# A three-layer graph network on one core: how far back a gather's hold reaches, ten or twelve gathered pairs

## The chip, the cores and the metric

The kernel runs on one core of one Trainium2 chip. The metric is the device time of one execution in microseconds, from launch to the last output written. The core's engines are TensorE (PE in the profile, PEld for its weight loads), VectorE (DVE), ScalarE (ACT), GpSimd (POOL) and SyncE (SP). Each has a queue of its own that it works through in order; they meet through semaphores. Transfers between the chip's memory (HBM) and the core's on-chip memory (SBUF) go through 16 DMA engines that all queues share. POOL issues the indirect transfers (an index for each row), SP and ACT the plain ones.

## The reference

N = 6250 nodes with D = 256 features, E = 100000 edges with 32 attributes and one of three types. The edges come sorted by their destination. Three layers follow each other, then a layernorm:

```python
ew = edge_attr @ edge_w + edge_b
rel_masks = [(edge_type == i).astype(x.dtype) for i in range(3)]
inv_cnt = [1.0 / jnp.maximum(segment_sum(m, dst), 1.0) for m in rel_masks]
for l in range(3):
    residual = x
    msg = relu(x[src] * ew)
    out = zeros((n, D))
    for i in range(3):
        h = segment_sum(msg * rel_masks[i][:, None], dst) * inv_cnt[i][:, None]
        out = out + h @ weights[l, i]
    out = out + x @ roots[l] + biases[l]
    x = residual + relu(out)
# result: layernorm(x_in + x)
```

`x[src]` is one row of 1 KB for each edge, in each of the three layers: this is what the gathers fetch.

## The kernel before

**Pairs and quads.** 128 edges are a tile, two tiles a pair (256 edges), two pairs a quad. There are 391 pairs. A pair is the unit of a step, a quad that of most DVE and ACT instructions. Pairs are numbered by u; a quad's number is q = u // 2, and i (0 or 1) is the tile within a pair.

**Layers and their order.** `layer()` writes out the program of one layer, once for each of the three. `order_of` lists the pairs in the order in which their sums are made. In layer 0 all 391 pairs are gathered. There, 26 quads (the destinations with the most edges, spread among the others) also write their edge weights into a table in HBM, `zone_table`, sorted anew. Layers 1 and 2 read these edges back sorted by source as 75 "lots" with plain loads, and gather only the other 339 pairs; they have 414 steps. `fetched` is the list of the gathered pairs in this order, and `nth[u]` is a pair's place in it.

**A step.** The loop over `it` (L1086) writes the instructions of all engines, and the engines keep this order. At step `it`, `pair(k)` is the pair k places ahead in the order. The parts that matter here, in the order in which they are written:

- `reduce(pair(0))`, L897 to L925: PE sums the pair's weighted rows into their nodes by a one-hot matrix. The last matmul of each tile is remembered as `summed[u, i]`.
- `gather(pair(AHEAD))`, AHEAD = 10: POOL gathers the rows of the pair ten steps ahead, with two indirect DMAs of 128 rows (L1458), one for each tile. The target is a "room" of SBUF for a quad; eight rooms (ROWS = 8, sixteen pairs) are used in turn. In layer 0 each gather is followed by a scatter of 128 rows into `zone_table` (L757), where one is waiting; there are 104, four for each of the 26 quads.
- `weigh` of the quad whose first pair is WEIGH = 2 steps ahead: DVE multiplies the gathered rows by the edge weights (L873), ACT applies the relu (L874). The last quad is done pair by pair and tile by tile (L873, L879).
- In layer 0, `keep_ew` one step before the weighing: ACT copies the quad's edge weights from PSUM into a buffer of the pool `keep` (three buffers, KEEP = 3), from L800 or L806. From there they go to HBM, by a plain store of SP or, for the 26 quads, by four scatters of POOL. A copy must wait until the buffer's last reader, a store or four scatters, is done with it.
- `seed_ew` (L821, L824) prepares the PSUM of a quad to come, in layers 1 and 2 from `ew_s`, which SP loads from HBM (L786, 128 rows of 4 KB). `take` (L930) copies a finished group of sums from PSUM, on ACT.

**What a gather waits for.** A gather raises one of POOL's eight semaphores, and so waits until the one eight before it has landed. Its room must be free, which means that the quad sixteen pairs back has been summed. Beyond these, `hold` adds a wait by hand for a sum that is more recent than the room requires:

```python
def hold(got, u, i):
    g = nth[u]
    if g >= LEAD + HEAD:
        behind(got, fetched[g - (LEAD if g >= 2 * LEAD else LEAD + HEAD)], i)
```

`behind(got, u, i)` makes the gather `got` wait for `summed[u, i]`. With LEAD = 10 and HEAD = 2 the first 12 gathered pairs of a layer have no hold, the next 8 wait for the sum twelve gathered pairs back, and from the 21st on for that ten back. `hold_early` does the same for the first EARLY = 8 pairs of layers 1 and 2, whose gathers stand at the end of the layer before (16 in each of these layers, listed as `src_e`); for these `fetched[nth[u] - LEAD]` counts back from the list's end. In layer 0 six pairs (FIRST) are gathered ahead of the loop.

Of the kernel before, what the change touches and what calls it, by code (L numbers as in the profile page):

```python
# [442 lines left out]
def ordered_path(ctx, tc, x, attr_laid, A, weights, roots, biases, edge_w, edge_b, out, src, src_i, seg, place_i, consts, x_root,  # L443
# [249 lines left out]
    def layer(l, r_sb, b_sb, ats, early, ready, pools):  # L693
# [46 lines left out]
# [5 lines that stand above are left out]
        def behind(got, u, i):  # L745
            tc.add_manual_dep(got.ins, summed[u, i].ins.name, mybir.DependencyInfo(
                mybir.DependencyClass.Sync, mybir.DependencyReason.DATA))

        def hold_early(got, u, i):
            behind(got, fetched[nth[u] - LEAD], i)  # L750

# [463 lines left out]
PARTS = 3  # L1215
FIRST = 6
EARLY = 8
LEAD = 10
HEAD = 2
READY = 2  # L1220
LOAD_EW = 10
# [465 lines left out]
```

## Time and profile before

| | |
|---|---|
| time, median of 3 runs | 3497.67 us |
| lowest and highest | 3482.07 and 3502.85 us |
| the profiled execution | 3495.29 us |
| its span, as the profile shows it | 3493.3 us |
| mean granted TensorE clock | 0.876 |
| gathers of layer 0 in the loop (L1458, `src_io`) | 770 |
| gathers of layers 1 and 2 in the loop (L1458, `src_r`) | 1324 |
| scatters of layer 0 (L757) | 104 |

The span is the time from the first to the last instruction that the profile recorded; the execution's own time has 2.0 us more around it. A busy time counts what an engine executes; the rest is waiting. For a group of instructions the profile gives the engine's idle time just ahead of them, split up by what ended it: "issue" is time in which nothing that the profile shows was waited for, a line with an engine is the instruction that came last by the semaphores, and "remote" is a semaphore whose origin the profile could not find.

### The profile page before, as it was taken

The page shows a single profiled execution, that of the slowest core. Times are in us where ns is not written, and L with a number is a line of the kernel's source. Part 1 is how long each engine was busy: PE and PEld are TensorE (multiplying, and loading weights), DVE is VectorE, ACT ScalarE, POOL GpSimd, SP SyncE. Part 2 cuts the span into 40 slices and gives each one's busy share as a digit, 9 for nine tenths or more (in the row PEclk, how much of TensorE's full clock was granted, in tenths as well). Part 3 has the DMA queues.
Part 4 walks back from the last instruction along what each step waited for, and adds up shares of the span by engine and source line. Part 5 has one row for each costly group of instructions (what it writes and reads, how often), then busy time and mean ns, then how long its engine had stood idle before and what let it go on. Part 6 is the DMA issues. An engine that isn't in the chain of part 4 may idle for free. (4 is left out here: it accounts for less than half of the span.)

```text
span 3493.3 us, 45265 instructions
## 1 busy us (share of the span) xinstructions
PE 2595.5 (74%) x12880; PEld 1999.6 (57%) x12880; DVE 1897.1 (54%) x4221; ACT 1891.7 (54%) x2580; POOL 2137.0 (61%) x2254
## 2 busy tenths in 40 slices
PE   5778777777777687777777777776777877778766
PEld 2445455555555455555566667665566666667665
DVE  6656555656555464444445555543445555566655
ACT  5666655555555555555554455554555655555555
POOL 6666666666666665666655566665666655565664
PEclk9889888888889899898988898888898999898888
DMA  7888555555555566767666676665776767766764
GB/s 247 274 261 257 189 179 182 177 174 174 173 172 173 165 194 220 229 215 223 211 202 205 203 224 216 216 212 160 257 235 219 230 220 223 227 215 222 225 216 153
DMA packets 358718, 730.97 MB, mean 209 GB/s; under 512 B 59082, under 2 KB 215804, under 8 KB 358332
## 3 DMA queue, kind: packets, MB, share of 16 engines
q1 hardware_dynamic: 243840, 426.68, 36.1%
q0 software_dynamic: 107616, 294.11, 28.4%
q10 hardware_dynamic: 7004, 7.19, 0.7%
q8 instruction: 107, 1.75, 0.2%
q14 instruction: 151, 1.24, 0.1%
HBM read 570.29 MB, written 157.46 MB: 208 GB/s over the span
## 5 line engine op out<-in xcount | busy, mean ns | idle before, releaser
L1458 POOL DMA_INDIRECT xs<-x_mid,src_r x1324 | 1255.9, 949 | 819.8 <-issue 396.8
L1458 POOL DMA_INDIRECT xs<-in_x_dram,src_io x770 | 734.3, 954 | 455.5 <-issue 161.8
L874 ACT ACTIVATE xs<-xs 128x1024 f32<-128x1024 f32 x533 | 560.4, 1051 | 767.1 <-DVE xs L873 484.5
L922 PE MATMUL h_p<-oh,xs 128*128 128x120 f32 x4608 | 716.1, 306 | 227.9 <-DVE acc L962 79.8
L922 PEld LDWEIGHTS h_p<-oh,xs 128*128 128x128 f32 x4608 | 671.7, 216 | 300.8 <-issue 115.7
L873 DVE TENSOR_TENSOR xs<-ew_p,xs 128x1024 f32<-128x1024 f32 x533 | 643.6, 1211 | 109.3 <-issue 48.9
L962 DVE TENSOR_TENSOR acc<-h_p,acc 128x240 f32 (+1 forms) x761 | 339.9, 449 | 662.7 <-remote 201.5
L991 PE MATMUL o_p<-w_sb,acc 128*128 128x256 f32 (+1 forms) x1752 | 505.3, 431 | 108.9 <-DVE acc L962 35.3
L991 PEld LDWEIGHTS o_p<-w_sb,acc 128*128 128x128 f32 (+1 forms) x1752 | 360.4, 216 | 209.9 <-issue 64.6
L914 PE MATMUL h_p<-xs,oh 128*120 128x256 f32 x1176 | 324.6, 409 | 80.9 <-ACT oh L886 24.9
L1022 DVE SCALAR_TENSOR_TENSOR x_root<-o_p,inv,x_root 128x256 f32<-128x256 f32 (+1 forms) x438 | 211.1, 482 | 303.4 <-PE o_p L991 93.3
L821 ACT ACTIVATE ew_p<-ew_s 128x1024 f32<-128x1024 f32 (+1 forms) x340 | 343.7, 1011 | 5.9 <-DMA ew_s<-ew_all 5.0
L914 PEld LDWEIGHTS h_p<-xs,oh 128*120 128x120 f32 x1176 | 222.6, 198 | 135.5 <-issue 50.4
L806 ACT ACTIVATE keep<-ew_p 128x1024 f32<-128x1024 f32 x170 | 172.4, 1014 | 202.0 <-remote 80.6
L850 PE MATMUL ew_p<-x_root,at 64*128 64x512 f32 x606 | 199.6, 738 | 79.1 <-issue 39.0
L911 PE MATMUL h_p<-xs,oh 128*120 128x257 f32 x772 | 213.4, 406 | 59.9 <-issue 36.6
L874 ACT ACTIVATE zone<-zone 128x1024 f32<-128x1024 f32 (+1 forms) x78 | 78.7, 1009 | 323.5 <-issue 156.6
L914 PE MATMUL h_p<-zone,oh 128*120 128x256 f32 x576 | 178.0, 447 | 99.8 <-ACT zone L874 36.8
L1008 ACT ACTIVATE acc<-zero_o 128x768 f32<-128x768 f32 (+1 forms) x150 | 141.4, 943 | 139.3 <-PE o_p L991 48.7
L836 PE MATMUL ew_p<-x_all,hot 128*128 128x256 f32 x588 | 164.5, 428 | 66.7 <-DVE hot L829 34.3
L890 DVE TENSOR_SCALAR oh<-iota_w,seg_o 128x120 f32<-128x120 f32 x782 | 207.8, 328 | 0.0
L911 PEld LDWEIGHTS h_p<-xs,oh 128*120 128x120 f32 x772 | 138.0, 191 | 109.3 <-issue 59.8
(182 smaller groups left out, 2870.3 us busy)
## 6 DMA issues: line engine op xcount, KB each, us to landing
ew_s<-ew_all SPq DMA_DIRECT2D x338, 512.0 KB
ew_all<-keep SPq DMA_DIRECT2D x169, 512.0 KB
oh_l<-oh_all SPq DMA_DIRECT2D x338, 120.0 KB
zone<-zone_table SPq DMA_DIRECT2D x72, 516.0 KB
xs<-x_mid,src_r POOLq DMA_INDIRECT x1324
oh_all<-oh_b SPq DMA_DIRECT2D x169, 120.0 KB
zone_table<-blank SPq DMA_DIRECT2D x21, 677.2 KB
x_mid<-x_all SPq DMA_DIRECT2D x98, 128.0 KB
```

The costliest lines, as they stand in the source:

```text
L821: nc.scalar.activation(ew_ps[q][:, :n], ew_ss[q][:, :n], AF.Copy)
L850: nc.tensor.matmul(ew_ps[q][:, k].rearrange("p i d -> p (i d)"), at[half, :], ew_sb[half].rearrange("p i d -> p (i d)"), start=False, stop ...
L873: nc.vector.tensor_mul(there, ew_ps[q][:, pairs.start:pairs.stop, :n], there)
L874: nc.scalar.activation(there, there, AF.Relu)
L890: nc.vector.tensor_scalar(ohs[q][:, i, :], iota_w[:, :, :WIN], at, None, op0=ALU.is_equal)
L911: summed[u, i] = nc.tensor.matmul(h_p[:WK, :D + 1], ohs[u // 2][:, t, :], wide[u // 2][:, u % 2, i, :], start=(i == 0 and first), stop=(i ...
L914: summed[u, i] = nc.tensor.matmul(h_p[:WK, :D], ohs[u // 2][:, t, :], rows_of(u, i), start=(i == 0 and first), stop=(i == n - 1 and closes ...
L922: summed[u, i] = nc.tensor.matmul(h_p[:, d * WK:(d + 1) * WK], rows_of(u, i)[:, d * P:(d + 1) * P] if d < DC else full_ones, (ohs if d < D ...
L962: nc.vector.tensor_tensor(there, h_ps[span][:, :CH * WK].rearrange("p (c r w) -> p c r w", c=CH, r=R), there, op=ALU.add)
L991: nc.tensor.matmul(o_p[:n, j, :], acc[:, d, r, slot:slot + n], w_sb[:, r * DC + d, :], start=(d == 0), stop=(d == DC - 1))
L1022: nc.vector.scalar_tensor_tensor(root, o_p[:n, j, :], inv[:n, c, r:r + 1], root, op0=ALU.mult, op1=ALU.add)
L1458: got = nc.gpsimd.indirect_dma_start(out=xs[:, u % 2, i, :], out_offset=None, in_=x_rows[:, :], in_offset=bass.IndirectOffsetOnAxis(ap=src ...
```

## The change

One number is changed. The hold now reaches twelve gathered pairs back from the 25th gathered pair of a layer on, in place of ten from the 21st on; before that it reaches fourteen back (LEAD + HEAD) in place of twelve, and the first 14 gathered pairs in place of 12 have none. In `hold_early` the sum waited for is two gathered pairs further back too. Rooms, steps and AHEAD stay as they are.

```diff
 EARLY = 8
-LEAD = 10
+LEAD = 12
 HEAD = 2
```

No instruction is added, removed or moved on any engine. What changes is what they wait for. In the rows below a name after "waits" is a semaphore: DMASW0 to DMASW7 are the landings of POOL's transfers, DMAHW those of SP's and ACT's, and PE, DVE, Activation the progress of an engine. Which value of it is waited for is not shown, so nearly all gathers read alike before and after, and two places show something. The first is POOL at the beginning of layer 0, around the gathers of the 13th and the 14th pair:

```order
 L1458 DMA xs<-in_x_dram,src_io 128x256 [waits DMASW6_49]
 L1458 DMA xs<-in_x_dram,src_io 128x256 [waits DMASW7_49]
-L1458 DMA xs<-in_x_dram,src_io 128x256 [waits DMASW0_49,PE_49]
-L1458 DMA xs<-in_x_dram,src_io 128x256 [waits DMASW1_49,PE_49]
-L1458 DMA xs<-in_x_dram,src_io 128x256 [waits DMASW2_49,PE_49]
-L1458 DMA xs<-in_x_dram,src_io 128x256 [waits DMASW3_49,PE_49]
+L1458 DMA xs<-in_x_dram,src_io 128x256 [waits DMASW0_49]
+L1458 DMA xs<-in_x_dram,src_io 128x256 [waits DMASW1_49]
+L1458 DMA xs<-in_x_dram,src_io 128x256 [waits DMASW2_49]
+L1458 DMA xs<-in_x_dram,src_io 128x256 [waits DMASW3_49]
 L1458 DMA xs<-in_x_dram,src_io 128x256 [waits DMASW4_49,PE_49]
 L1458 DMA xs<-in_x_dram,src_io 128x256 [waits DMASW5_49,PE_49]
```

These four gathers no longer wait for a sum; they stand in the same place.

The second is ACT in layer 0, behind one of the 26 quads whose weights are scattered: the third and the fourth copy into `keep` after that quad's own (both L806 here). Before:

```order
L806 ACTIVATE keep<-ew_p 128x1024 [waits DMAHW3_49,PE_49,Activation_49]
L824 ACTIVATE ew_p<-x_root 128x1024
L930 ACTIVATE h_s<-h_p 120x257 [waits PE_49]
L874 ACTIVATE xs<-xs 128x4x256 [waits DMASW6_49,DMASW5_49,DMASW7_49,DMASW4_49,DVE_49]
L893 ACTIVATE oh_b<-oh 128x480 [waits DVE_49]
L806 ACTIVATE keep<-ew_p 128x1024 [waits DMASW3_49,DMASW5_49,DMASW1_49,DMASW7_49,PE_49,Activation_49]
```

And with the change:

```order
L806 ACTIVATE keep<-ew_p 128x1024 [waits DMASW3_49,DMASW5_49,DMASW1_49,DMASW7_49,PE_49,Activation_49]
L824 ACTIVATE ew_p<-x_root 128x1024
L930 ACTIVATE h_s<-h_p 120x257 [waits PE_49]
L874 ACTIVATE xs<-xs 128x4x256 [waits DMASW6_49,DMASW4_49,DVE_49]
L893 ACTIVATE oh_b<-oh 128x480 [waits DVE_49]
L806 ACTIVATE keep<-ew_p 128x1024 [waits DMAHW3_49,PE_49,Activation_49]
```

The two copies have exchanged their buffers: now the third waits for the four scatters (DMASW3, 5, 1, 7) and the fourth for the plain store (DMAHW3). This is so behind 16 of the 26 quads.

## Rows read from the trace of the kernel before

**Rows 1.** The page: busy us, share of the span, instructions, by engine.

```profile
...
PE 2595.5 (74%) x12880; PEld 1999.6 (57%) x12880; DVE 1897.1 (54%) x4221; ACT 1891.7 (54%) x2580; POOL 2137.0 (61%) x2254
```

**Rows 2.** POOL by form: busy us, mean ns | idle before, what ended it.

```profile
...
L1458 POOL DMA_INDIRECT xs<-x_mid,src_r x1324 | 1255.9, 949 | 819.8 <-issue 396.8 <-PE h_p L914 142.5 <-remote 76.5
L1458 POOL DMA_INDIRECT xs<-in_x_dram,src_io x770 | 734.3, 954 | 455.5 <-issue 161.8 <-PE h_p L922 113.8 <-remote 68.7
```

**Rows 3.** Line L1458: ns min/median/max, starts; idle until (us, times); who waited.

```profile
...
L1458 POOL DMA_INDIRECT xs<-x_mid,src_r x1324: 940/946/1371, 1381.0 to 3467.7; - x190
L1458 POOL DMA_INDIRECT xs<-in_x_dram,src_io x770: 940/946/2079, 22.4 to 1344.8; - x193
...
  PE h_p L922: 167.9, 157
  remote: 149.4, 105
  PE h_p L914: 143.1, 119
...
  ACT xs L874: 10.4, 5
  DVE xs L873: 9.4, 7
  PE h_p L914: 5.6, 2
```

**Rows 4.** POOL timeline, last gathers: start us, us [idle before <-releaser].

```profile
...
3457.70 0.94 POOL L1458 DMA_INDIRECT xs<-x_mid,src_r  x1 [1.54 <-PE h_p L914]
...
3462.02 0.95 POOL L1458 DMA_INDIRECT xs<-x_mid,src_r  x1 [0.31 <-issue]
3464.00 0.94 POOL L1458 DMA_INDIRECT xs<-x_mid,src_r  x1 [1.04 <-PE h_p L914]
...
3466.50 0.95 POOL L1458 DMA_INDIRECT xs<-x_mid,src_r  x1 [0.30 <-issue]
3467.75 0.94 POOL L1458 DMA_INDIRECT xs<-x_mid,src_r  x1 [0.30 <-issue]
```

**Rows 5.** Timeline of DVE, the last three weighings; x2 joins two instructions.

```profile
...
3471.99 2.35 DVE L873 TENSOR_TENSOR xs<-ew_p,xs 128x1024 f32<-128x1024 f32 x2
...
3478.34 0.68 DVE L873 TENSOR_TENSOR xs<-ew_p,xs 128x512 f32<-128x512 f32 x1
3478.94 0.75 DVE L879 TENSOR_TENSOR xs<-ew_p,xs 128x256 f32<-128x256 f32 x2
```

**Rows 6.** Chain of waits 2520 to 3494 us: shares, then start, us of pieces.

```profile
...
by line: issue 19.6%; PE h_p L914 13.2%; PE h_p L922 11.9%; PE o_p L991 10.7%; PE ew_p L836 6.1%; another core or an unknown queue 4.7%; DVE xs L873 3.6%; PE r_p L975 3.2%; DVE x_root L1022 3.2%; DMA xs<-x_mid,src_r 2.5%; POOL xs L1458 2.4%
...
3059.38 2.59 DMA xs<-x_mid,src_r
...
3134.77 5.07 DMA xs<-x_mid,src_r
```

**Rows 7.** Timeline of POOL around two scattered quads of layer 0.

```profile
...
633.93 0.98 POOL L757 DMA_INDIRECT zone_table<-keep,slot_i  x1 [0.30 <-issue]
...
1236.50 0.97 POOL L1458 DMA_INDIRECT xs<-in_x_dram,src_io  x1 [1.70 <-remote]
...
1240.52 0.98 POOL L757 DMA_INDIRECT zone_table<-keep,slot_i  x1 [0.30 <-issue]
```

**Rows 8.** Timeline of ACT, the third copies into keep behind these quads.

```profile
...
643.70 1.02 ACT L806 ACTIVATE keep<-ew_p 128x1024 f32<-128x1024 f32 x1 [5.97 <-remote]
...
1243.76 1.02 ACT L806 ACTIVATE keep<-ew_p 128x1024 f32<-128x1024 f32 x1 [1.18 <-PE ew_p L850]
```

**Rows 9.** Line L786, the edge weights' loads: who waited for them (us, times).

```profile
...
  ACT zone L874: 9.2, 3
  ACT ew_p L821: 5.0, 2
  DVE zone L873: 2.6, 1
```

## The prediction, made before the change was run

> **What bounds the kernel now.** I read the page's busy times first. No engine is full: PE 74%, POOL 61%, DVE and ACT 54% [rows 1]. The kernel is a pipeline of steps, one pair of edge tiles each, in which PE, DVE and ACT wait for one another. So the question is only whether the gathers, POOL's work, are ever what the others wait for.
>
> Second, POOL's own rows. Its two large groups are 1324 + 770 = 2094 gathers of about 0.95 us [rows 2]. Between two that wait for nothing 0.30 us pass (gaps marked "issue" in the timeline [rows 4]), so POOL can issue one in 1.25 us and a pair in 2.5 us. The layers use them more slowly: 770 gathers between 22.4 and 1344.8 us are 3.43 us a pair, and 1340 (1324 and the 16 early ones of the last layer) between 1381.0 and 3467.7 us are 3.11 us a pair [rows 3]. POOL therefore has time left, and spends it waiting. Its idle time before the two groups is 819.8 + 455.5 = 1275 us [rows 2]; 2094 x 0.30 = 628 us of it is that fixed gap, which leaves 647 us of real waiting. The view of the gather's line puts most of it down to the sums on PE (the two largest 167.9 and 143.1 us) and to "remote", 149.4 us [rows 3]. So the hold that the change loosens does bind now: POOL runs at the end of its leash.
>
> Third, the other side: who waits for a gather? The same view shows ACT 10.4, DVE 9.4 and PE 5.6 us, 25.4 us in 14 waits [rows 3]; its other rows are smaller than these, so I count 30 us, 0.9% of the span. That is all that an earlier gather could give back directly, if each of them is real.
>
> They are probably not real. At the end of the program gathers and uses can be counted back against each other. The last two gathers start at 3466.50 and 3467.75 us [rows 4] and belong to the last pair, which DVE weighs at 3478.94 (L879); the two before (3464.00, 3465.25) belong to the half quad weighed at 3478.34, the four from 3457.70 to 3462.02 to the second of the two weighings that begin at 3471.99 [rows 5], that is at about 3473.1. The chain of waits shows seven gathers from start to landing in its part of the last layer, between 2.59 and 5.07 us [rows 6]. So the data of these quads lie there 3478.94 - 3467.75 - 5.07 = 6.1 us before their use at the worst, and 3473.1 - 3462.02 - 5.07 = 6.0 us for the other. The general reason is the order of the program: a pair's gather is issued at ten steps before its sum, its weighing two steps before, so eight steps of 3.1 us, 25 us, lie between, less what POOL needs to get there. A gather that starts 3 to 5 us before the weighing it is said to release, as the chain has it, would be one issued one or two steps ahead. Such instructions wait for several semaphores, which later gathers also raise.
>
> **The change part by part.** *The hold.* Gathers of every layer from the 25th pair on wait for a sum two pairs further back, so POOL may run two pairs, 2 x 3.1 to 2 x 3.4 = 6 to 7 us, further ahead. No instruction is added or removed. POOL's waiting does not go away: the number of gathers per step is set by the steps. Once per layer, POOL gets four gathers (5.0 us) ahead, and then waits for PE as before. What is late next on POOL is therefore the same sum, two pairs back; the landing of the eighth gather back, which every gather also waits for, is four pairs away and needs at most 5.07 us, and the room of 16 pairs back is still behind the hold of twelve. On PE, DVE and ACT this costs nothing, and gives back between 0 and 30 us. I take 0, as the counted quads have 6 us to spare.
>
> *The layers' beginnings.* In layer 0 four gathers lose their wait for PE altogether (the first order fence). They come at a place where the data are early too: layer 0's gathers start at 22.4 us and go at POOL's own rate. 0 us. The early gathers of layers 1 and 2 move two pairs back from the end of the layer before, but wait for the landing of x_mid; 0 us.
>
> *The scatters.* In layer 0 they stand in POOL's queue behind gathers and so are moved with them. A gather ahead of a scatter now waits up to 1.70 us for its sum [rows 7]; with the change it waits for an older one, and the four scatters of a quad are done earlier by about that. Behind the scatters are only gathers, which have time. 0 us, a gain of nothing since ACT's copies are not known to wait for them.
>
> *The copies into keep.* The order shows a side effect: at 16 of 26 quads in layer 0 ACT's third copy after a scattered quad now waits for its four scatters, and the fourth for the plain store, where it was the other way round. ACT is in order: behind that copy are the next seed (L824), the take (L930) and the relu (L874), for which PE and DVE wait. In the trace of before the last scatter starts at 633.93 us and the third copy runs at 643.70: 9.8 us, nearly twice the longest landing. A tight place has 1240.52 and 1243.76 us, 3.24 us [rows 7, 8], and there a landing of 2.59 to 5.07 us (those of gathers on the same queue; a scatter's is not shown) would hold ACT for 0 to 1.83 us. The bounds for 16 places are 0 and 16 x 1.83 = 29 us; I take 0, nearer to the ordinary place.
>
> **The sum** is 0, between -30 and +29 us against the profiled execution's 3495.3 us (its span is 3493.3, 2.0 us lie around it). That execution is 2.4 us below the median of the three runs, 3497.7, which themselves lie 20.8 us apart, so I give **3496 us**, with 3465 to 3525 for the case itself. About 1%, 35 us, is what a measurement of this kernel can tell from no change.
>
> **The rivals.** *Gathers are on the path.* If the chain is right, its last layer holds seven landings of gathers, 2.5% of the stretch from 2520 us, and gathers on POOL with 2.4% [rows 6], together 4.9% of 974 us = 48 us. Two pairs (6 us) more would cover every one of the landings. That gives 3448 us, and 3350 if the two layers that the chain doesn't reach are the same. For it: POOL waits 647 us, most of it on the hold. Against it: the counted quads, and that DVE's waits show only 9.4 us on gathers in all three layers. Chance 0.09.
>
> *ACT waits for scatters* (slower). Place: the 16 exchanged copies in layer 0. If POOL gets to the scatters later by the time of one pair with its two scatters, 5.1 us, than in that tight place, each third copy waits 1.83 + 5.1 = 6.9 us, which is 110 us and 3606 us. It decides from 35/16 = 2.2 us a place on. For it: ACT already idles 5.97 us before such a third copy, a wait whose cause the view calls "remote" [rows 8]. Against it: POOL's queue is in the same order and each of its waits ends earlier, not later. Chance 0.08.
>
> *Gathers crowd the loads.* While PE is behind, POOL may issue four gathers more before it stops. A gather moves 128 rows of 1 KB, four of them as much as one ew_s load (128 rows of 4 KB). What busy queues add to a transfer I take from the spread of the gathers' own landings, 5.07 - 2.59 = 2.5 us [rows 6]. The loads' landings are waited for 9.2 + 5.0 + 2.6 = 16.8 us, in 6 waits [rows 9]. If these get 2.5 us longer, it is +15 us, 3511 us; slower by over 1% takes 14 such loads on the path. Against it: the rate of the gathers stays, so in the mean nothing more is in the queues. Chance 0.07. [...]
>
> **How the numbers follow.** Forecast 0.76, gathers on the path 0.09, scatters 0.08, crowding 0.07. The forecast and the crowding together are 0.83, so the range is theirs: 3465 to 3525, widened by the 10 us by which the three runs differ from their middle: **3455 to 3535 us**. Faster by over 1%: 0.09 and 0.02 of the forecast, 0.11. Slower: 0.08, 0.02 of the crowding and 0.02 of the forecast, 0.12. Within 1%: 0.77.
>
> **What would show it.** Right: POOL's idle time before its two large groups stays near 1275 us, still put down to PE's sums; the last gathers of the program start 6 us further ahead of their weighings (16 us in place of 10); the waits for the gather's line stay under 30 us; ACT's idle before its copies into keep changes by less than 30 us. Wrong: DVE's idle time falls by tens of us with POOL's unchanged (gathers were on the path); the copies idle 35 us or more longer, with scatters as what ended it; or the waits for L786 rise from 16.8 us to over 50. I would also be wrong if the steps themselves go faster or slower by the way that transfers and sums meet, which none of these views shows.

## The result and the profile after

With the hold of twelve the kernel takes 3529.07 us (median of 12 runs) against 3497.38 us before (12 runs): ratio 1.0095, 95% interval 1.007 to 1.012. It is slower by some 32 us. The profiled execution takes 3529.12 us, its span is 3527.3 us, its mean granted clock 0.866 (0.876 before).

The page's busy times of the changed kernel, which answer to [rows 1]:

```profile
PE 2606.9 (74%) x12880; PEld 2004.8 (57%) x12880; DVE 1898.5 (54%) x4221; ACT 1890.8 (54%) x2580; POOL 2136.0 (61%) x2254
```

No engine does more: DVE, ACT and POOL are within 1.4 us of before, PE is 11 us up. What is added is waiting. POOL's groups by form, for [rows 2], with the scatters as a third row:

```profile
L1458 POOL DMA_INDIRECT xs<-x_mid,src_r x1324 | 1255.8, 948 | 820.9 <-issue 437.5 <-PE h_p L914 118.1 <-remote 77.9
L1458 POOL DMA_INDIRECT xs<-in_x_dram,src_io x770 | 733.4, 953 | 437.6 <-issue 167.7 <-remote 77.1 <-PE h_p L922 76.5
L757 POOL DMA_INDIRECT zone_table<-keep,slot_i x104 | 102.0, 981 | 70.0 <-ACT keep L800 39.8 <-issue 24.4 <-ACT ew_p L824 4.6
```

POOL's idle time ahead of the gathers is 1258.5 us, as forecast (1275 before). The third row is new: POOL now stands 39.8 us at the scatters until ACT has made the copy that they take away (L800); before, no wait for that copy was among the first releasers of the row:

```profile
L757 POOL DMA_INDIRECT zone_table<-keep,slot_i x104 | 102.0, 981 | 31.7 <-issue 28.6 <-ACT keep L806 1.2 <-ACT oh_b L893 1.2
```

The view of the gathers' line, for [rows 3], three of its releasers first, then who waited:

```profile
  remote: 157.2, 103
  PE h_p L922: 143.5, 139
  PE h_p L914: 118.7, 104
...
  DVE xs L873: 18.9, 7
  ACT xs L874: 11.5, 6
  DVE xs L867: 10.6, 2
```

The three largest waits for gathers come to 41.0 us, where the prediction had named under 30 us as a sign of being right. They don't follow the hold, though: `e4_lead_only` below, with twelve, has 24.5 us in all, and `e3_turn_only`, with ten, 52.0 us.

The last gathers and weighings, for [rows 4, 5], on POOL's timeline and DVE's:

```profile
3494.91 0.94 POOL L1458 DMA_INDIRECT xs<-x_mid,src_r  x1 [0.33 <-PE h_p L914]
3496.16 0.95 POOL L1458 DMA_INDIRECT xs<-x_mid,src_r  x1 [0.30 <-DVE acc L962]
```

```profile
3512.43 0.68 DVE L873 TENSOR_TENSOR xs<-ew_p,xs 128x512 f32<-128x512 f32 x1
3513.03 0.75 DVE L879 TENSOR_TENSOR xs<-ew_p,xs 128x256 f32<-128x256 f32 x2
```

The last pair is gathered 3513.03 - 3496.16 = 16.9 us ahead of its weighing, 11.2 us before: the change does what it says. The loads' waits, for [rows 9], have not grown:

```profile
  ACT zone L874: 7.1, 2
  ACT ew_p L821: 5.1, 1
```

The gathers, then, are earlier, and nothing that hangs on their data or on the loads is seen to explain 32 us. Where the time goes shows from the weighings on DVE, 620 in each trace and the same ones: I compare the starts of the 4th, the 41st (layer 0 under way), the 197th (layer 1), the 409th (layer 2) and the last.

| trace | 4th starts at | 41st to 197th | 197th to 409th | 409th to last |
|---|---|---|---|---|
| before | 48.6 us | 1099.9 us | 1062.3 us | 1053.4 us |
| changed | 49.2 us | 1125.0 us | 1051.0 us | 1069.8 us |

The loss lies in layer 0 and layer 2. But one trace each is not enough for that, since stages of this length differ by 14 to 24 us between traces of kernels that are alike in them (below).

### The profile page after: what moved, and what is told of

It is laid out like the page before. It is cut to its first block, busy times and chain, and to the rows that moved or that the text cites. A ratio compares the mean times of both kernels' runs of the same rounds, so it can differ in the third digit from the quotient of the medians.

```text
span 3527.3 us, 45230 instructions
## 1 busy us (share of the span) xinstructions
PE 2606.9 (74%) x12880; PEld 2004.8 (57%) x12880; DVE 1898.5 (54%) x4221; ACT 1890.8 (54%) x2580; POOL 2136.0 (61%) x2254
## 4 chain that ended last, share of the span: by engine, by line
PE 49%; issue 19%; DVE 11%; another core or an unknown queue 8%; ACT 6%; DMA 3%; POOL 2%; DVEq 1%; ACTq 0%; POOLq 0%; SPq 0%
PE h_p L922 12%; PE o_p L991 9%; PE h_p L914 9%; PE ew_p L850 5%; PE h_p L911 3%; PE ew_p L836 3%; PE r_p L975 3%; DVE xs L873 3%; DMA xs<-x_mid,src_r 2%; POOL xs L1458 2%; DVE x_root L1022 2%; DVE oh L890 2%; PE h_p L934 2%; DVE acc L962 1%
## 5 line engine op out<-in xcount | busy, mean ns | idle before, releaser
L1458 POOL DMA_INDIRECT xs<-x_mid,src_r x1324 | 1255.8, 948 | 820.9 <-issue 437.5
L1458 POOL DMA_INDIRECT xs<-in_x_dram,src_io x770 | 733.4, 953 | 437.6 <-issue 167.7
L922 PE MATMUL h_p<-oh,xs 128*128 128x120 f32 x4608 | 718.1, 307 | 208.2 <-issue 72.7
L922 PEld LDWEIGHTS h_p<-oh,xs 128*128 128x128 f32 x4608 | 671.9, 216 | 284.2 <-issue 99.1
L914 PE MATMUL h_p<-xs,oh 128*120 128x256 f32 x1176 | 324.9, 409 | 71.8 <-ACT oh L886 24.8
L914 PEld LDWEIGHTS h_p<-xs,oh 128*120 128x120 f32 x1176 | 221.1, 197 | 125.6 <-issue 42.4
L806 ACT ACTIVATE keep<-ew_p 128x1024 f32<-128x1024 f32 x170 | 172.3, 1013 | 208.5 <-remote 79.4
L911 PE MATMUL h_p<-xs,oh 128*120 128x257 f32 x772 | 215.6, 408 | 76.3 <-issue 39.2
L914 PE MATMUL h_p<-zone,oh 128*120 128x256 f32 x576 | 177.7, 446 | 89.1 <-DVE acc L962 41.0
L911 PEld LDWEIGHTS h_p<-xs,oh 128*120 128x120 f32 x772 | 138.9, 193 | 126.1 <-issue 61.0
```

Of the source, the lines that this page charges most:

```text
L911: summed[u, i] = nc.tensor.matmul(h_p[:WK, :D + 1], ohs[u // 2][:, t, :], wide[u // 2][:, u % 2, i, :], start=(i == 0 and first), stop=(i ...
L914: summed[u, i] = nc.tensor.matmul(h_p[:WK, :D], ohs[u // 2][:, t, :], rows_of(u, i), start=(i == 0 and first), stop=(i == n - 1 and closes ...
L922: summed[u, i] = nc.tensor.matmul(h_p[:, d * WK:(d + 1) * WK], rows_of(u, i)[:, d * P:(d + 1) * P] if d < DC else full_ones, (ohs if d < D ...
L1458: got = nc.gpsimd.indirect_dma_start(out=xs[:, u % 2, i, :], out_offset=None, in_=x_rows[:, :], in_offset=bass.IndirectOffsetOnAxis(ap=src ...
```

## The experiments

Kernels that are compared below ran on the same chip as the kernel before, and the chips differ: on three of them (and for the result above) the kernel before takes 3493 to 3540 us, on two 2884 and 2887 us. The first kind is the one to explain; the second turned out to be a test by itself.

### Which part of the change costs

Theory A: the buffers of `keep`. The addresses that the program gives them show more than the waits did: before, 32 of the 196 copies (two at each of 16 places) do not take the buffer whose turn it is; with the change all 196 go strictly in turn. Theory B: the longer lead costs by itself in layer 0. Theory C: the longer lead crowds the loads, in layers 1 and 2. In `e1_layer0` and `e2_layers12` the hold differs by layer:

```diff
-            if g >= LEAD + HEAD:
+            lead = LEAD if l else LEAD_0
+            if g >= lead + HEAD:
```

with 12 in layer 0 alone, or 12 in layers 1 and 2 alone. In `e3_turn_only` (hold of ten) and `e4_lead_only` (hold of twelve) three buffers are taken by a written list instead of from the pool (one of the lines changed):

```diff
...
-                there = early_pool.tile([P, 2, 2, D + 2], F32, name="keep", bufs=KEEP)
+                there = keep_room()      # kept[KEPT[n]], n counts the copies
```

The list is that of the changed kernel in `e3_turn_only`, that of the kernel before in `e4_lead_only`; ACT's waits then read as in the one or the other.

> Hold of twelve in layer 0 alone; layers 1 and 2 as before (ten). The copies into keep take their three buffers strictly in turn, as in the changed kernel. Theory A (the buffers' order: ACT's copies meet the scatters) and theory B (a longer lead costs by itself in layer 0, where POOL now waits 39.8 us for keep copies at the scatters) both give most of the change, 3520 to 3530 us, ratio 1.007 to 1.009. Theory C (the longer lead crowds the loads in layers 1 and 2): 3495 to 3502, ratio below 1.002.

> Hold of twelve in layers 1 and 2 alone; layer 0 as before. Theories A and B: nothing or a few us, 3495 to 3505, ratio 0.999 to 1.003. Theory C: most of the change, 3520 to 3530.

> Hold of ten everywhere; the three keep buffers are taken strictly in turn, as in the changed kernel (written out as a list). Theory A: the whole loss of layer 0, 3518 to 3530, ratio 1.006 to 1.009. Theories B and C: as before, 3490 to 3503.

> Hold of twelve everywhere; the keep buffers in the order of the kernel before (written out as a list), so that behind the scattered quads the third copy does not wait for the scatters at 16 places. Theory A: as before, 3490 to 3505. Theories B and C: as the changed kernel, 3520 to 3535, ratio 1.007 to 1.011.

Measured, against 3493.4 us before: `e1_layer0` 3508.0 us, 1.005 (1.002 to 1.008); `e2_layers12` 3517.8 us, 1.0056 (1.0028 to 1.0084); `e3_turn_only` 3497.7 us, 1.0013 (0.999 to 1.0036); `e4_lead_only` 3531.0 us, 1.0104 (1.0068 to 1.0139). Theory A is out: the buffers alone change nothing that can be told, and the hold alone has the whole loss. B and C each held half of it, and each missed the time that it expected: layer 0 and layers 1 and 2 lose about 0.5% each. What they don't say is how.

### What the longer hold meets

The beginning of layer 0 is the cleanest place, since all traces are alike there up to 41 us. POOL, ACT and PE in the kernel before, and below them in `e4_lead_only` (its lines are 7 or 8 higher: the copy is L813, the gather L1466):

```profile
41.49 0.94 POOL L1458 DMA_INDIRECT xs<-in_x_dram,src_io  x1 [0.31 <-issue]
43.03 0.95 POOL L1458 DMA_INDIRECT xs<-in_x_dram,src_io  x1 [0.60 <-remote]
45.57 0.95 POOL L1458 DMA_INDIRECT xs<-in_x_dram,src_io  x1 [1.59 <-remote]
```

```profile
47.54 1.02 ACT L806 ACTIVATE keep<-ew_p 128x1024 f32<-128x1024 f32 x1 [7.61 <-issue]
```

```profile
40.66 0.17 PE L917 MATMUL h_p<-full_ones,oh_b 128*120 128x1 bf16 x1
```

```profile
41.41 0.95 POOL L1466 DMA_INDIRECT xs<-in_x_dram,src_io  x1 [0.30 <-issue]
...
47.67 0.95 POOL L1466 DMA_INDIRECT xs<-in_x_dram,src_io  x1 [0.30 <-issue]
52.08 0.94 POOL L1466 DMA_INDIRECT xs<-in_x_dram,src_io  x1 [3.46 <-remote]
```

```profile
51.95 1.02 ACT L813 ACTIVATE keep<-ew_p 128x1024 f32<-128x1024 f32 x1 [12.10 <-issue]
```

```profile
40.59 0.17 PE L924 MATMUL h_p<-full_ones,oh_b 128*120 128x1 bf16 x1
```

In both, PE's last recorded matmul before the copy is over by 40.8 us, and ACT's copy waits for nothing but such a matmul (the landings recorded of the plain store that it also waits for lie before 30 us). It runs at 47.54 us in the one and 51.95 us in the other. What differs is POOL: with ten it stops for sums from 43 us on; with twelve it issues five more gathers at its own rate of 1.25 us (42.66 to 47.67), and stops then. In both, ACT's wait ends only after POOL has stopped. The trace's semaphore records (which the views above don't print) hold raises of PE's semaphore: in `e4_lead_only` one at 46.9 us, while POOL still issues, then six between 51.8 and 52.1 us. Two matmuls of a sum last 0.67 us in their records, so that all but the last of these six were probably done before, and signalled late. Theory D: while POOL issues one gather behind the other, PE's finished work is signalled late, and what the hold really does is to make POOL pause.

The same records bear this out for PE over the whole program, but not in its strictest form. For each recorded raise I take the time since the end of PE's last record that raises this semaphore. In the 14 traces of the slower kind of chip 27 to 29% of PE's raises come more than 1 us after it, the latest 8.7 to 14 us with a hold of eight to twelve and 19 us with fourteen; in the six of the faster kind it is 0.1%, and for ACT and DVE at most 0.2% on both kinds. (On the slower kind a fifth of PE's raises and about half of the others' are not in the trace: before the change 20% of PE's, 46% of DVE's and 51% of ACT's.) Inside stretches of six or more gathers and scatters without a pause, from 2.5 us on, PE's raises are half as frequent as in the whole trace, 0.40 against 0.78 a us before the change. So they are thinned out there, not stopped. Part of this goes the other way round, since it is a raise of PE that ends many of POOL's waits (338 before the change, for the sums of L911, L914 and L922); that POOL's stretch comes first rests on the beginnings compared here and below.

Four runs against theory D. `d8` and `d14` change LEAD to 8 and 14; for eight the gather is also written at `pair(8)` instead of `pair(10)`, because a sum must stand in the program before the gather that waits for it, and the scatters come two pairs earlier among the gathers by that, so that `d8` differs by more than the hold. `m_pool` keeps POOL busy without gathers, `m_load` makes traffic without POOL:

```diff
+                if l == 0 and nth[u] == 14:          # m_pool
...
+                    for _ in range(12):
+                        nc.gpsimd.iota(spare, pattern=[[1, 512]], base=0, channel_multiplier=0)
```

```diff
+                if l == 0 and nth[u] == 13:          # m_load
...
+                    for k in range(16):
+                        nc.sync.dma_start(spare[k % 5], x[k * P:(k + 1) * P, :P])
```

> Hold of eight gathered pairs (ten at the beginning of a layer) in place of ten; the gathers are written eight steps ahead in place of ten, so that the sum that a gather waits for stands before it. Theory D (while POOL issues one gather behind the other without a pause, PE's finished sums are signalled late, and the hold sets how long such a stretch gets): faster than before, 3465 to 3490, ratio 0.992 to 0.998; the fourth weighing of layer 0 starts before 46.0 us (46.0, 46.0 and 48.6 us in the three traces with ten, 49.2, 52.7 and 53.0 in those with twelve). Theory E (ten is right because gathers with less lead come too late): slower than before by 10 us or more, with waits for the gathers of over 60 us.

> Hold of fourteen (sixteen at the beginning), which is nearly the room's own sixteen. Theory D: slower again, 3545 to 3570, ratio 1.014 to 1.022; at the start eight more gathers pass without a wait than with ten, 10 us, so that the fourth weighing starts at 55 to 58 us. Theory F (the loss is one of landing at another phase of the steps, not of how long POOL goes on): no order in the three, 3490 to 3530; the fourth weighing at 49 to 53 us as with twelve.

> The kernel before with twelve writes of a 128x512 ramp on POOL ahead of the first gather that waits for a sum (the 15th pair's): POOL is busy for 6 us or more there, and issues no gather. If it is POOL's being busy that holds up PE's signals, the fourth weighing starts at 50 us or later. If it is the gathers, it starts at 46.0 to 48.6 us as in the traces with ten.

> The kernel before with sixteen plain loads of 128 rows of 512 bytes by SP, which has nothing else to do there, from about 40 us on: traffic into SBUF like that of the gathers, but not from POOL. If it is traffic that holds up PE, the fourth weighing starts at 50 us or later. If it is POOL's gathers alone, at 46.0 to 48.6 us.

Measured, against 3496.0 us before: `d8` 3487.7 us, 0.9988 (0.996 to 1.0015); `d14` 3677.1 us, 1.0501 (1.0468 to 1.0534); `m_pool` 3497.1 us and `m_load` 3488.9 us, one execution each. The fourth weighing on DVE, in this order: `d8`, `m_pool`, `m_load`:

```profile
40.49 1.23 DVE L873 TENSOR_TENSOR xs<-ew_p,xs 128x1024 f32<-128x1024 f32 x1 [2.45 <-DMA xs<-in_x_dram,src_io]
```

```profile
46.09 1.22 DVE L877 TENSOR_TENSOR xs<-ew_p,xs 128x1024 f32<-128x1024 f32 x1 [5.16 <-ACT keep L810]
```

```profile
49.37 1.23 DVE L877 TENSOR_TENSOR xs<-ew_p,xs 128x1024 f32<-128x1024 f32 x1 [7.94 <-ACT keep L810]
```

It starts at 40.5 us with eight, 46.0 to 48.6 with ten, 49.2 to 53.0 with twelve and 59.8 us in `d14`: the order that D asks for, the last 1.8 us later than it expected. POOL's being busy is not the cause: in `m_pool` its ramps run from 42.72 to 50.15 us, and ACT's copy, which waits for PE, is made in the middle of them, at 45.03 us. `m_load` is not clear, 0.8 us above the traces with ten, whose own spread is 2.6 us; plain traffic may have a small share, and whether it is the issuing of the gathers or their transfers was not separated. As to the whole time, D was wrong for eight, which gains nothing that can be told, and far too low for fourteen: +181 us, where it expected +50 to +75. Theory E (late data with eight) and F (no order) are out.

The table of stages says where fourteen loses:

| hold in the stage | 41st to 197th (layer 0) | 197th to 409th | 409th to last |
|---|---|---|---|
| eight (1 trace) | 1100.1 us | 1046.6 us | 1064.6 us |
| ten (5) | 1093.7 to 1108.1 | 1038.5 to 1062.3 | 1053.4 to 1070.9 |
| twelve (3) | 1115.6 to 1125.0 | 1045.2 to 1054.9 | 1069.6 to 1072.3 |
| fourteen (1) | 1253.9 | 1053.7 | 1081.9 |

Layer 0 has 154 us of it, and layer 0 alone has scatters. POOL's row for these in `d14`:

```profile
L757 POOL DMA_INDIRECT zone_table<-keep,slot_i x104 | 102.4, 985 | 216.5 <-ACT keep L800 169.3 <-ACT ew_p L824 23.5 <-issue 20.7
```

The gathers that come late behind them are not seen to cost it: all waits for gathers together are 42.2 us in this trace, 31.7 us before. One such place in `d14`, on POOL, ACT, PE and DVE:

```profile
662.09 0.96 POOL L1458 DMA_INDIRECT xs<-in_x_dram,src_io  x1 [0.53 <-DVE xs L873]
669.80 0.98 POOL L757 DMA_INDIRECT zone_table<-keep,slot_i  x1 [6.75 <-ACT keep L800]
...
680.06 0.94 POOL L1458 DMA_INDIRECT xs<-in_x_dram,src_io  x1 [0.30 <-PE h_p L911]
...
690.08 0.95 POOL L1458 DMA_INDIRECT xs<-in_x_dram,src_io  x1 [0.30 <-issue]
694.08 0.95 POOL L1458 DMA_INDIRECT xs<-in_x_dram,src_io  x1 [3.05 <-remote]
```

```profile
668.20 1.01 ACT L800 ACTIVATE keep<-ew_p 128x1024 f32<-128x1024 f32 x1
...
693.89 0.39 ACT L930 ACTIVATE h_s<-h_p 120x257 f32<-120x257 f32 x1 [12.09 <-remote]
```

```profile
681.85 1.13 PE L850 MATMUL ew_p<-x_root,at 64*128 64x512 f32 x4 [1.08 <-issue]
694.33 0.66 PE L934 MATMUL h_p<-ident_o,h_s 120*128 120x120 f32 x2 [11.35 <-issue]
```

```profile
691.04 1.00 DVE L1022 SCALAR_TENSOR_TENSOR x_root<-o_p,inv,x_root 128x256 f32<-128x256 f32 x2 [12.29 <-remote]
```

POOL comes to the scatter 6.75 us before it can issue it, and stands there for ACT's copy. It then has what it missed to make up for: 17 gathers and scatters from 669.80 to 690.08 us, without a pause, the last nine of them gathers. In these, PE's last records are over by 683 us; DVE, ACT and, through them, PE wait 11 to 12 us, and go on 1.0 to 4.3 us after the last gather's start; no raise of PE is recorded from 679.8 to 691.0 us. Theory D2: in layer 0 the longer hold brings POOL to the scatters before the copies, and the long stretch that follows costs the time.

### The scatters, and a pause

In `d12_late` and `d14_late` a scatter is issued two or four steps later in POOL's queue, as much as the hold is longer (the lines that note a copy's step are left out):

```diff
...
-            if waiting:
-                there, q, k, i = waiting.pop(0)
+            if waiting and it_is[0] > waiting[0][-1] + LATE:    # 2 with twelve, 4 with fourteen
+                there, q, k, i, _ = waiting.pop(0)
```

In `d14_pause` (fourteen) and `d10_pause` (ten) POOL writes two ramps of 128x512 ahead of every eighth gather of layer 0.

> Hold of fourteen, and each scatter of layer 0 stands four steps later in POOL's queue than before, so that POOL meets it when its copy into keep has been made. Theory D2 (with a longer hold POOL waits at the scatters for ACT's copies, 169.3 us with fourteen, and then makes up for it in a stretch of gathers without a pause, in which PE's signals are held up): most of the 145 us that layer 0 loses with fourteen comes back, 3530 to 3590 us, ratio 1.01 to 1.027; POOL's wait for the copies below 40 us. Rival G (the lead alone does it, the scatters only make POOL wait where it has time): 3650 to 3680.

> Hold of fourteen, and in layer 0 POOL writes two ramps of 128x512 (0.63 us each) ahead of every eighth gather, which breaks its stretches of gathers without taking any away. Theory D (stretches without a pause hold up PE): faster than fourteen alone (3677) by 30 us or more, 3560 to 3650, though POOL has 120 us more to do. Rival H (what is lost is POOL's own time: it comes late behind the scatters): slower than fourteen alone, 3690 or more.

> The change (twelve), and each scatter of layer 0 two steps later in POOL's queue. Theory D2: the 15 us that the body of layer 0 loses with twelve come back, 3505 to 3517 us, ratio 1.003 to 1.006 (layer 2 and the start stay). Rival G: 3525 to 3533 as with twelve.

> The kernel before (ten) with the same ramps ahead of every eighth gather in layer 0. Theory D: the stretches are held short by the sums already, and a few us come back or nothing: 3475 to 3497. Rival H: slower, 3505 or more.

These four fell on the other kind of chip, where the kernel before takes 2883.8 us: `d14_late` 1.0 (0.9991 to 1.001), `d12_late` 0.9993 (0.9982 to 1.0003), `d14_pause` 1.0324 (1.0308 to 1.034), `d10_pause` 1.0341 (1.0327 to 1.0355). None of the times in the expectations could be met there, and of the rivals only H has its sign: on this chip 192 ramps of 0.56 us and their gaps cost 90 to 96 us, with ten as with fourteen. Three of the kernels were measured again on another chip, with `d14` beside them:

> The same kernel as d14_late (hold of fourteen, scatters four steps later). On a chip on which the kernel before takes about 2884 us, all three theories: ratio 0.998 to 1.002. On one on which it takes about 3495 us, theory D2 (POOL waits at the scatters for copies, then makes up for it in one long stretch of gathers): ratio 1.01 to 1.027, with the loss of layer 0 mostly gone. Rival G (the lead alone, the scatters are nothing): 1.044 to 1.055.

> The same kernel as d14_pause (hold of fourteen, two ramps on POOL ahead of every eighth gather of layer 0). Where the kernel before takes about 2884 us: 1.03 again, by POOL's own time. Where it takes about 3495 us, theory D (stretches of gathers without a pause hold up PE's signals): 1.02 to 1.042, less than fourteen alone (1.050). Rival H (POOL's own time): 1.055 or more.

> The same kernel as d12_late (twelve, scatters two steps later). Where the kernel before takes about 2884 us: 0.998 to 1.002. Where it takes about 3495 us, theory D2: the 15 us of layer 0's body come back, 1.003 to 1.006. Rival G: 1.008 to 1.011 as with twelve.

> The same kernel as d14 (hold of fourteen, nothing else). Where the kernel before takes about 3495 us: 1.050 again. Where it takes about 2884 us and no late bunches of PE signals are seen, theory D: 0.998 to 1.006, since there is nothing that a longer stretch of gathers could hold up. Rival G: 1.03 or more there too.

This chip was of the first kind (3540.1 us before): `d14_2` 1.0479 (1.0441 to 1.0517), `d14_late2` 1.0115 (1.008 to 1.0151), `d12_late2` 1.0059 (1.0032 to 1.0086), `d14_pause2` 1.0439 (1.0393 to 1.0484). So the scatters' place gives back 127 of the 163 us that fourteen costs; layer 0's stage goes from 1255.7 to 1122.4 us, and POOL's row for the scatters in `d14_late2` reads:

```profile
L757 POOL DMA_INDIRECT zone_table<-keep,slot_i x104 | 102.2, 983 | 31.7 <-issue 28.6 <-ACT keep L806 1.5 <-ACT xs L874 0.6
```

The first half of D2, that the scatters' place costs the time, is shown for fourteen. For twelve it is not: the same edit lies where D2 put it (1.0059 against 1.0095), but the two intervals overlap, and layer 0's stage in its trace, 1119.6 us, is not below that of twelve (1115.6 to 1125.0), though on a chip on which the kernel before takes 1.2% longer. The second half, that it costs by the long stretch, is not shown either. I counted in layer 0, from 41 us on, the stretches of 14 or more gathers and scatters whose starts follow each other within 1.4 us:

| kernel | stretches of 14 or more |
|---|---|
| ten (5 traces) | 0, in one trace 1 |
| twelve (3) | 6 to 8 |
| fourteen (`d14`, `d14_2`) | 26 and 25 |
| scatters later (`d12_late2`, `d14_late2`) | 0 |
| fourteen with pauses (`d14_pause2`) | 0, the longest has 11 |

With fourteen the stretches go together with the loss when the scatters are moved. But with twelve they go and the stage stays as long, and with the pauses they are gone and layer 0's stage is still 1232.1 us, 24 us under `d14_2`; in the whole, 12 us came back in the medians (1.0439 against 1.0479, intervals overlapping), so that the pause missed its expectation. The ramps also take POOL's own time, though, 108.3 us in this trace, and no run separates the two. At the beginning of the program, where no scatter is near, the pause does what D says: two ramps put two gathers' starts 2.31 us apart in place of 1.25, and the fourth weighing starts at 41.70 us in place of 54.5 and 59.8 us. POOL and DVE in `d14_pause2`:

```profile
37.30 0.95 POOL L1467 DMA_INDIRECT xs<-in_x_dram,src_io  x1 [0.30 <-issue]
38.26 1.20 POOL L741 IOTA ramp<- 128x512 int32 x2
39.61 0.95 POOL L1467 DMA_INDIRECT xs<-in_x_dram,src_io  x1 [0.15 <-issue]
```

```profile
41.70 1.23 DVE L882 TENSOR_TENSOR xs<-ew_p,xs 128x1024 f32<-128x1024 f32 x1 [0.40 <-issue]
```

Why the pauses don't pay over the whole layer stays open; POOL still waits 147.2 us at the scatters in that trace.

The last two kernels are 14 in layers 1 and 2 alone (the edit of `e2_layers12`), and the change once more:

> Hold of fourteen in layers 1 and 2 alone, layer 0 as before (ten). Theory D2 (the 5% of fourteen are layer 0's scatters; what is left in layers 1 and 2 grows slowly with the hold): where the kernel before takes about 3500 us, 1.006 to 1.011. Rival G (the lead alone, everywhere): 1.02 or more. On a chip on which the kernel before takes 2884 us: 0.998 to 1.002.

> The change itself once more. Where the kernel before takes about 3500 us: 1.007 to 1.012 as measured. Where it takes about 2884 us and PE's signals come without late bunches, theory D: 0.998 to 1.003; rival G: 1.007 to 1.012 there too.

They fell on a chip of the second kind (2886.6 us before): `e5_14_layers12` 0.996 (0.9945 to 0.9975), a little faster than any theory expected there, `d12_2` 0.9984 (0.9973 to 0.9996), as D expected. There the change costs nothing, and the longer hold gains a little, as its plain reading would have it. What fourteen costs in layers 1 and 2 alone on the first kind was not measured; in `d14` and `d14_late2` layer 2's stage is 20 and 24 us above the mean with ten (1062 us), the second on a slower chip. The page of `d12_2`, part 1, and its gathers:

```profile
PE 2397.6 (83%) x12880; PEld 1862.6 (65%) x12880; DVE 1895.2 (66%) x4221; ACT 1882.7 (65%) x2580; POOL 2142.7 (74%) x2254
...
L1458 POOL DMA_INDIRECT xs<-x_mid,src_r x1324 | 1259.2, 951 | 424.3 <-issue 190.3
```

The same instructions with the same busy time on DVE, ACT and POOL within 8 us, 646 us sooner than the changed kernel's profile on the first kind. PE is busy for 209 us less, with a mean granted clock of 0.944 against 0.866; the rest is waiting. The fourth weighing starts at 40.65 us there, and in all six traces of this kind between 40.5 and 41.7 us, whatever the hold.

## Why the prediction failed

It was right on the gathers. They are not on the path; their data came 6 us further ahead (16.9 us against 11.2, which the prediction's last lines put at 10); POOL's waiting did not go away; the loads did not get later (12.2 us of waits for them against 16.8); and the exchange of the keep buffers, which the order shows and which had a rival of its own, costs nothing that can be told (`e3_turn_only`, 1.0013). The rivals "ACT waits for scatters" and "gathers crowd the loads" had the sign, but not the mechanism: with the buffers' order of before the whole loss is there, and the waits for the loads did not grow. The forecast of no change does not hold, since the interval lies clear of 1. That the measured time is inside the stated range, 6 us below its end, and just inside 1%, is luck: the range was made of costs that did not occur.

Two steps failed.

- "On PE, DVE and ACT this costs nothing, and gives back between 0 and 30 us." The step took the hold for a leash that binds POOL and nobody else, and so put its loosening at nothing or a gain. Loosening it alone costs 38 us (`e4_lead_only`, 3531.0 against 3493.4 us). At the program's beginning the runs show that PE's results come through in the pauses which it forces on POOL (the fourth weighing starts at 46.0 to 48.6 us with ten, at 49.2 to 53.0 with twelve); that the same makes up the loss over the whole of a layer is likely, but not shown. Where the price lies is known roughly. By the stages it is about 19 us in layer 0 (1119 against 1100 us in the mean), 8 us in layer 2 (1071 against 1062 us, with ranges that overlap), and about 2 us at the beginning (the 41st weighing at 269 against 267 us), while layer 1 shows none. By the whole times it is 15 us for layer 0 and 24 us for layers 1 and 2 (`e1_layer0`, `e2_layers12`). In layers 1 and 2 the long stretches are about as few with twelve as with ten (3 or 4 of 14 or more against 1 or 2), so that what costs there stays open.
- "... the four scatters of a quad are done earlier by about that. Behind the scatters are only gathers, which have time." The step asked who waits behind the scatters, and not what the scatters wait for. Moved two pairs ahead in time, they stand before ACT's copy, 39.8 us in all; the gathers behind them do have time, but they are then issued in one long stretch (6 to 8 of 14 or more in layer 0, with ten at most 1). With fourteen the scatters' place costs 127 of 163 us; with twelve its share is not shown.

The trace of before had the first in it. The ACT row at 47.54 us waits 7.61 us for matmuls that PE's records end at 40.83 us, and it goes on just where POOL's timeline has its first real gaps (1.59 us before the gather at 45.57 us, 1.25 us before that at 47.77 us). The prediction's last sentence, that the steps might change "by the way that transfers and sums meet, which none of these views shows", names the place but goes too far in its last half: POOL's timeline beside ACT's waits, another view of the same trace, hints at it.

The granted clock moved too, from 0.876 to 0.866 in the profiles; on one chip its mean is 0.876 over 29 runs of the kernel before and 0.870 over six of `e4_lead_only`. Among these 29 runs the slower ones mostly have the lower clock (correlation of time and clock -0.67; -0.41 over 17 runs of the kernel before on another chip, -0.19 over 17 on a third). Which of the two follows the other no run shows, and none separates a share of its own.

What stays open: by what way PE's signals come late while gathers follow each other, and why on some chips alone. In the traces of the second kind of chip next to none are late (0.1% of PE's raises, 2884 us). On the first kind, in the place read in `d14`, engines wait 11 to 12 us behind nine gathers in a row; what holds them up no run shows.

## What to carry to other kernels

A wait that holds back an engine with time to spare may serve another one (shown here for the program's beginning): before it is loosened, look at what the other engines do in the moments in which the held engine pauses. When a queue is let run ahead, go through all that stands in it, and ask of each what it waits for, not only who waits for it: issuing the scatters four steps later undid most of a 5% loss (127 of 163 us). And a tuning number such as this hold can be right on one chip and wrong, or idle, on the next (the change measured 1.0095 on one, 0.9984 on another); compare on more than one before it is fixed.

## What the runs showed of the hardware

- The kernel before takes 2884 and 2887 us on two chips and 3493 to 3540 us on three. Two profiles of the changed kernel, one on each kind, lie 646 us apart with the same busy time of DVE, ACT and POOL within about 8 us; of the 646 us PE's busy time has 209 us, at a granted clock of 0.944 against 0.866; the rest is waiting.
- On the slower kind (14 traces), 27 to 29% of PE's recorded semaphore raises come more than 1 us after the last PE record that makes one; on the faster kind (six) 0.1%, and ACT's and DVE's at most 0.2% on both. While indirect gathers follow each other every 1.25 us, PE's raises are about half as frequent as in the whole trace (0.40 against 0.78 a us before the change, which is on the slower kind); in the place read in `d14` the engines went on 1.0 to 4.3 us after the last gather's start. At the program's beginning one distance of 2.31 us between two gathers' starts was enough in `d14_pause2`: the fourth weighing started at 41.7 us, in place of 54.5 and 59.8. POOL's own arithmetic did not have this effect there (7.4 us of ramps in `m_pool`, the fourth weighing at 46.1 us); whether plain loads have some was not settled (49.4 against 46.0 to 48.6 us).
- Stages of a thousand microseconds differ by 14 to 24 us between five traces of kernels that are the same in them, so that a loss of 0.5% must be measured, and is not read from one pair of traces.
